# The last twenty microseconds of a two-layer graph and expert network: halves, another order, and two sums on TensorE

## The chip, the cores and the metric

The kernel runs on one core of a Trainium2 chip. The metric is the device time of one launch in microseconds, the median of a few runs. Five engines work side by side, each with its own instruction stream: TensorE (PE, matrix products into PSUM), VectorE (DVE), ScalarE (ACT), GpSimd (POOL) and SyncE (SP, which here only issues DMAs). DMAs issued by SP, ACT and GpSimd run on the core's 16 DMA engines. Semaphores order the engines; a scheduler that knows which instruction reads and writes which tile places the waits.

## The reference

3327 nodes have 256 features each; an adjacency matrix of 3327 x 3327 says which are connected. There are two layers. In each, a normalized `x` goes through a graph step (layer 0 takes the mean of the neighbours, layer 1 weights them by attention) that is added to `x`, and then through a mixture of experts that is added too. In layer 1 the expert part is:

```python
h1 = relu(einsum('bsd,edh->bseh', features, expert_w1) + expert_b1)      # 6 experts, 256 x 256
h2 = relu(einsum('bseh,ehf->bsef', h1, expert_w2) + expert_b2)
expert_out = einsum('bsef,efo->bseo', h2, expert_w3) + expert_b3
sel = take_along_axis(expert_out, top_i[:, :, :, None], axis=2)           # the two best experts of each node
combined = sum(sel * routing_weights[..., None], axis=2)
x = x + combined
```

All is float32. Only two of six experts count for a node, and the kernel computes only those.

## The kernel before

Rows are handled in tiles of 128: 26 tiles, of which the last (tile 25) has 127 rows. `CHUNKS` are groups of four tiles: six whole ones (tiles 0 to 23) and one of two (tiles 24 and 25). `xs` holds `x` of all tiles in SBUF for the whole run.

The stages in time are the graph step of layer 0, its experts, the graph step of layer 1, and its experts. In the expert stage a node's row appears twice, once for each of its experts. The rows of an expert are taken in *slots* of 256 rows. For a slot GpSimd gathers the rows (`rows_in`, line 601), TensorE transposes them (`turned`, line 618), and two layers follow (`layer1`, line 1306, with ScalarE's ReLU at line 1309). `out1` is the third: eight matmul records (four float32 matmuls, two records each) write both 128-row halves `h` of a PSUM tile `ps` (line 1318), VectorE adds the bias `b3` to the whole tile (line 1321) and multiplies each half by the rows' routing weights (line 1323). `rows_out` (line 627) lets GpSimd scatter the two halves with one indirect DMA each into a DRAM array `zd`. `zd` has 2 rows of 256 numbers a node, one for each of its experts. `slots1` is the loop over the slots; `USUAL1` is the number of slots that the data usually needs (29), and if it needs more, a conditional block (`with more(...)`, line 1428) that is usually skipped runs the rest.

The end of the kernel adds up `x` and both rows of `zd`. `results` (line 647) loads a piece of `zd` on SP's queue into a tile `z` of [128, tiles, 2, 256]; `summed` (line 657) lets VectorE add `xs` to the first row, and then the second row to it, both in place; `stored` (lines 662 and 666) writes the sum to the output, and splits the tile of 127 rows into 112 and 15 rows (`last_rows`). `LOW`, the first four chunks (tiles 0 to 15), is done while the last slots still run, because the rows of those nodes are written early. The other ten tiles (16 to 25) follow the last slot: lines 1435 to 1439. They are five pieces of two tiles, 512 KB each, loaded, added and stored in the order of the tiles, the loads on SP's queue and the stores on ACT's.

Every engine keeps the order in which its instructions are given out. Within the code behind the conditional block the order is that of the program. Loads of `zd` wait for all scatters into it, and for what GpSimd does on the skipped block. Whoever reads a PSUM tile waits for the matmuls that write it. `bank(c, shape)` (line 607) takes a tile of one of three pools of PSUM, each with two buffers; a [128, 2, 256] float32 tile takes a whole bank. `ident` is the 128 x 128 identity that the transposes use too.

Of the kernel before, what the change touches and what calls it, by code (L numbers as in the profile page):

```python
# [9 lines left out]
F32 = mybir.dt.float32  # L10
# [5 lines left out]
OP = mybir.AluOpType  # L16
# [3 lines left out]
P = 128  # L20
# [5 lines left out]
def kernel(  # L26
# [26 lines left out]
    nc = tc.nc  # L53
    N, D = x.shape
# [7 lines left out]
    BT = 4  # L62
    CHUNKS = [list(range(t, min(t + BT, NT))) for t in range(0, NT, BT)]
# [8 lines left out]
    def last_rows():  # L72

        n = N - NF * P
        return [(lo, hi) for lo, hi in ((0, n // 16 * 16), (n // 16 * 16, n)) if lo < hi]
# [12 lines left out]
    USUAL1 = min(SLOTS1, int(2 * N / S1 + E1 / 2 + (E1 / 12) ** 0.5))  # L88
    LATE1 = USUAL1 - E1
    KNOWN1 = [n - 4 for n in EARLY1]  # L90
    LOW = CHUNKS[: 4 * len(CHUNKS) // 7]
# [25 lines left out]
    xs = keep.tile([P, NT, D], F32, name="xs")  # L117
# [22 lines left out]
    ident = const.tile([P, P], F32, name="ident")  # L140
# [99 lines left out]
    last = {}  # L240
# [366 lines left out]
    def bank(c, shape):  # L607

        return ps_c[c].tile(shape, F32, name=f"acc{c}") if c >= 0 else ps_mm.tile(shape, F32, name="mm")
# [13 lines left out]
    def rows_out(s, who, y):  # L623
        n = who.shape[1]
        for h in range(n):
            with in_turn_on_pool():
                last["pool"] = nc.gpsimd.indirect_dma_start(  # L627
                    out=zviews[n * s + h], out_offset=bass.IndirectOffsetOnAxis(ap=who[:, h, 0:1], axis=0),
                    in_=y[:, h, :], in_offset=None, bounds_check=2 * NP - 1, oob_is_err=False,
                )  # L630
            if s < LATE1:
                z_ready.append(last["pool"].ins.name)

    def weight(who, h):

        return who.bitcast(F32)[:, h, 2:3]
# [3 lines left out]
    def results(blk, zp, low=None, z=None, behind=(), step=BT):  # L640

        z = zp.tile([P, BT, 2, D], F32, name="z") if z is None else z
        of, case = (zd, {}) if low is None else (zd_low, dict(cond=low, bounds_check="skip_entire_dma"))
        for i in range(0, len(blk), step):
            part = blk[i : i + step]
            n, t0 = len(part), part[0]
            ins = nc.sync.dma_start(z[:, i : i + n], of[2 * t0 * P : 2 * (t0 + n) * P, :].rearrange("(t p k) d -> p t k d", p=P, k=2), **case)  # L647
            if low is not None:
                for name in (*z_ready, *behind):
                    tc.add_manual_dep(ins.ins, name, mybir.DependencyInfo(mybir.DependencyClass.Sync, mybir.DependencyReason.DATA))  # L650
        return z

    def summed(blk, z):

        n, t0 = len(blk), blk[0]
        for k in range(2):
            nc.vector.tensor_tensor(z[:, :n, 0, :], z[:, :n, k, :], z[:, :n, 0, :] if k else xs[:, t0 : t0 + n, :], op=OP.add)  # L657

    def stored(engine, blk, z):
        full = [t for t in blk if t < NF]  # L660
        if full:
            engine.dma_start(
                out[full[0] * P : (full[-1] + 1) * P, :].rearrange("(t p) d -> p t d", p=P), z[:, : len(full), 0, :]
            )
        for lo, hi in last_rows() if blk[-1] >= NF else ():
            engine.dma_start(out[NF * P + lo : NF * P + hi, :], z[lo:hi, len(full), 0, :])
# [300 lines left out]
    early = {}  # L967
# [30 lines left out]
    WB, BB = 3 * 2 * H1, 3 * 2 * H1 + D  # L998
# [110 lines left out]
    who = {}  # L1109
# [186 lines left out]
    def weights1(s, i):  # L1296
        return early["w"][s % 3][:, i * 2 * H1 : (i + 1) * 2 * H1].rearrange("p (k h) -> p k h", k=2)
# [15 lines left out]
    def out1(s, who, h2):  # L1313
        ps = bank(1 if s < EARLY1[1] else 0, [P, 2, D])
        w = weights1(s, 2)
        for h in range(2):
            for c in range(NC1):
                nc.tensor.matmul(ps[:, h, :], h2[:, c, h * P : (h + 1) * P], w[:, c, :],  # L1318
                                 start=(c == 0), stop=(c == NC1 - 1))
        y = early["io"].tile([P, 2, D], F32, name="y", bufs=5)  # L1320
        nc.vector.tensor_tensor(y, ps, early["w"][s % 3][:, None, WB:BB].to_broadcast([P, 2, D]), op=OP.add)  # L1321
        for h in range(2):
            last["dve"] = nc.vector.tensor_scalar(y[:, h, :], y[:, h, :], weight(who, h), None, op0=OP.mult)  # L1323
        outs.append(lambda: rows_out(s, who, y))

    outs = []
    who = {}
    xg, xT, h1, h2, zs = {}, {}, {}, {}, {}
# [14 lines left out]
    def slots1(first, end):  # L1343
        for s in range(first - 3, end + 1):
            if first <= s - 1 < end:
                out1(s - 1, who[s - 1], h2.pop(s - 1))
# [76 lines left out]
    tail = ctx.enter_context(tc.tile_pool(name="tail", bufs=len(CHUNKS)))  # L1423
# [4 lines left out]
    with more(*early["more"]):  # L1428
        list(slots1(USUAL1, SLOTS1))
        for blk in LOW:  # L1430
            z = results(blk, tail)
            summed(blk, z)
            stored(nc.scalar, blk, z)

    zs = [(blk, results(blk, tail, step=2)) for blk in CHUNKS[len(LOW) :]]
    for blk, z in zs:
        for i in range(0, len(blk), 2):
            summed(blk[i : i + 2], z[:, i : i + 2])
            stored(nc.scalar, blk[i : i + 2], z[:, i : i + 2])


# [33 lines left out]
```

## Time and profile before

| | |
|---|---|
| Median of 3 runs | 1002.71 us (1001.34, 1002.71, 1010.84) |
| Profiled execution: time, span | 1003.3 us, 1000.3 us |
| PE busy | 923.2 us, 92% of the span |
| PE weight loads, DVE, ACT, POOL busy | 777.1, 485.0, 280.9, 434.8 us |
| Mean granted clock of TensorE | 0.975 |
| DMA | 200.56 MB, 200 GB/s in the mean; 386 GB/s from 988 to 994.5 us |
| The last slot's matmuls end | 979.1 us |
| The five loads of `zd` are issued | 985.87 to 988.3 us |
| VectorE's adds of the last pieces | 989.60 to 996.60 us |

The span runs from the first to the last instruction of the profiled execution; the time is that of the whole launch, 3.0 us more. Busy time is time in which an engine computes; waiting, and issuing a DMA, are not counted. TensorE is busy almost throughout, but not in the last 21 us, in which it does nothing at all; a share of the whole span says nothing of that stretch. The chain of waits follows what ended last back from step to step. The granted clock is the share of full speed at which TensorE was allowed to run: 1.00 or 0.50 in the stretches of this trace.

### The profile page before, as it was taken

Reading aid. Unit: us, or ns where it says so; the run is one execution under the profiler, and the core shown is the slowest. Engines: PE = TensorE matmul, PEld = TensorE weight load, DVE = VectorE, ACT = ScalarE, POOL = GpSimd, SP = SyncE. Lnnn points to the kernel's source line nnn. Section 1 sums busy time; section 2 is a strip of 40 time slices with the busy share of each in tenths; the row PEclk is TensorE's granted clock in tenths of the full one; section 3 lists DMA queues with packets and bytes.
Section 4 is the critical chain, followed back from the end, with each engine's and each line's share of the span. In section 5 each row is a group of like instructions: output and inputs, shape, how many; then the busy total and the mean of one; then the engine's idle time right before and its main releaser. Section 6 shows DMA issues by size and latency. Waiting matters only on the chain. (4 is left out here: it accounts for less than half of the span.)

```text
span 1000.3 us, 14311 instructions
## 1 busy us (share of the span) xinstructions
PE 923.2 (92%) x4506; PEld 777.1 (78%) x4506; DVE 485.0 (48%) x1788; ACT 280.9 (28%) x634; POOL 434.8 (43%) x407
## 2 busy tenths in 40 slices
PE   7889999989997999999999999999999898789981
PEld 5777878779896999888988687777787787678870
DVE  7564585245622332212122687576666563435563
ACT  3311321035311111111111444152141643234420
POOL 2040052532576455454545311000634677677751
PEclk9999999999999999999999999999999999889986
DMA  9989667856666656567888398988973223242376
GB/s 337 335 277 317 217 177 252 255 173 214 189 159 169 201 157 147 167 191 212 226 268 273 57 320 292 305 276 317 244 215 85 65 75 64 44 102 90 96 253 209
DMA packets 104945, 200.56 MB, mean 200 GB/s; under 512 B 30436, under 2 KB 59558, under 8 KB 104864
## 3 DMA queue, kind: packets, MB, share of 16 engines
q1 hardware_dynamic: 64002, 150.87, 46.1%
q0 software_dynamic: 20528, 30.56, 14.2%
q10 hardware_dynamic: 20334, 18.17, 5.7%
q8 instruction: 36, 0.59, 0.3%
q14 instruction: 45, 0.37, 0.2%
HBM read 170.39 MB, written 35.47 MB: 206 GB/s over the span
## 5 line engine op out<-in xcount | busy, mean ns | idle before, releaser
L831 PE MATMUL acc<-big,y 128*128 128x512 f32 (+2 forms) x1456 | 337.3, 385 | 21.9 <-ACT y L887 7.5
L831 PEld LDWEIGHTS acc<-big,y 128*128 128x128 f32 (+1 forms) x1456 | 260.4, 190 | 79.1 <-issue 8.6
L1065 PE MATMUL acc<-xT,w 128*128 128x256 f32 (+3 forms) x1024 | 211.0, 359 | 0.0
L1065 PEld LDWEIGHTS acc<-xT,w 128*128 128x128 f32 x1024 | 184.0, 198 | 15.8 <-issue 3.5
L384 POOL DMA_INDIRECT list<-where,t_idx x104 | 111.2, 1069 | 155.2 <-DVE t_idx L381 97.0
L705 DVE TENSOR_SCALAR big<-adj 128x1536 fp32r<-128x1536 int32 (+5 forms) x128 | 111.0, 871 | 100.5 <-DMA adj<-in_adj_t 61.5
L1088 PE MATMUL acc<-w,hid 128*128 128x256 f32 (+3 forms) x512 | 118.0, 381 | 0.0
L1095 POOL DMA_INDIRECT xd<-y,who x44 | 68.2, 1550 | 98.9 <-DVE y L1093 53.9
L1073 DVE TENSOR_TENSOR hid<-hid,acc 128x512 f32<-128x512 f32 (+3 forms) x64 | 40.0, 625 | 143.9 <-PE acc L1065 134.8
L1088 PEld LDWEIGHTS acc<-w,hid 128*128 128x128 f32 (+3 forms) x512 | 88.9, 177 | 20.2 <-issue 3.6
L1069 ACT ACTIVATE hid<-acc 128x512 f32<-128x512 f32 (+3 forms) x64 | 35.0, 547 | 202.0 <-PE acc L1065 190.5
L1309 ACT ACTIVATE h<-acc,v 128x256 f32<-128x256 f32 x116 | 54.8, 473 | 93.8 <-PE acc L1306 93.3
L601 POOL DMA_INDIRECT xg<-hd,who x58 | 63.3, 1092 | 40.3 <-issue 35.1
L627 POOL DMA_INDIRECT zd<-y,who x58 | 67.2, 1159 | 29.6 <-issue 12.2
L1306 PE MATMUL acc<-h,v 128*128 128x256 f32 x232 | 61.1, 386 | 1.7 <-ACT h L1309 1.7
L1318 PE MATMUL acc<-v,h 128*128 128x256 f32 x232 | 61.5, 412 | 0.1
L1306 PE MATMUL acc<-xT,v 128*128 128x256 f32 x232 | 61.0, 385 | 0.0
L289 POOL TENSOR_TENSOR ln_var<-ln_var,half 128x2 f32<-128x2 f32 (+2 forms) x19 | 15.9, 839 | 101.1 <-DVE ln_var L287 87.7
L1095 POOL DMA_INDIRECT xd<-y,whos x20 | 32.2, 1612 | 57.8 <-DVE y L1093 43.3
L1321 DVE TENSOR_TENSOR y<-acc,v 128x512 f32<-128x512 f32 x29 | 20.0, 691 | 73.8 <-PE acc L1318 73.8
L1306 PEld LDWEIGHTS acc<-h,v 128*128 128x128 f32 x232 | 44.5, 199 | 9.0 <-ACT h L1309 2.5
L1318 PEld LDWEIGHTS acc<-v,h 128*128 128x128 f32 x232 | 46.3, 210 | 6.6 <-ACTq L575 0.5
(300 smaller groups left out, 987.7 us busy)
## 6 DMA issues: line engine op xcount, KB each, us to landing
adj<-in_adj_t SPq DMA_DIRECT2D x58, 768.0 KB
w<-in_ffn_w SPq DMA_DIRECT2D x78, 512.0 KB
adj<-in_adj_t SPq DMA_DIRECT2D x25, 639.5 KB
adj<-in_adj_t SPq DMA_DIRECT2D x25, 512.0 KB
adj<-in_adj_t SPq DMA_DIRECT2D x12, 767.0 KB
hd<-ln_h ACTq DMA_DIRECT2D x12, 512.0 KB
w_all<-w1d SPq DMA_DIRECT2D x6, 898.0 KB
w1d<-in_ffn_w ACTq DMA_DIRECT2D x18, 256.0 KB
```

The source lines that it names most:

```text
L384: ins = nc.gpsimd.indirect_dma_start(out=rows_of[2 * (t0 + j) + i], out_offset=bass.IndirectOffsetOnAxis(ap=idx[:, i, j : j + 1], axis=0), ...
L601: last["pool"] = nc.gpsimd.indirect_dma_start(out=xg[:, h, :], out_offset=None, in_=of, in_offset=bass.IndirectOffsetOnAxis(ap=who[:, h, 1 ...
L627: last["pool"] = nc.gpsimd.indirect_dma_start(out=zviews[n * s + h], out_offset=bass.IndirectOffsetOnAxis(ap=who[:, h, 0:1], axis=0), in_= ...
L705: last["mask"] = nc.vector.tensor_scalar(mask[:kr, :, :cols], a[:kr, :, :cols], value, None, op0=op)
L831: last["graph"] = nc.tensor.matmul(acc[c][k][:, :w], y[:kr, j, part, k * P : (k + 1) * P], mask[:kr, jj, i0 : i0 + w], start=(j == 0 and p ...
L1065: last["slot"] = nc.tensor.matmul(q[:, c, :n], w[:, k, h0 : h0 + 2 * P - 1 : 2], xT[:, k, :n], start=(k == 0), stop=(k == KD - 1))
L1073: last["silu"], last["hid"] = silu, nc.vector.tensor_mul(hid[:, :, :n], hid[:, :, :n], ps[1][:, :, :n])
L1088: nc.tensor.matmul(ps[:m, h, :], hid[c // 2][:, c % 2, h * P : h * P + m], w3[:, c // 2, c % 2, :], start=(c == 0), stop=(c == NC0 - 1))
L1095: ins = last["pool"] = nc.gpsimd.indirect_dma_start(out=xd_of[2 + h] if s < USUAL0 else xd, out_offset=bass.IndirectOffsetOnAxis(ap=who[s] ...
L1306: ins = nc.tensor.matmul(ps[:, c, :], w[:, k, c : H1 : NC1], src[:, k, :], start=(k == 0), stop=(k == 1))
L1309: last["act"] = nc.scalar.activation(dst[:, c, :], ps[:, c, :], AF.Relu, bias=early["w"][s % 3][:, BB + 2 * i + c : BB + 2 * i + c + 1])
L1318: nc.tensor.matmul(ps[:, h, :], h2[:, c, h * P : (h + 1) * P], w[:, c, :], start=(c == 0), stop=(c == NC1 - 1))
```

## The change

Two places change. In `out1`, for the last usual slot only, the bias add is done in halves, each followed by its half's weighting. At the end, the ten last tiles are taken in another order: the piece with tiles 24 and 25 first, then 20 and 21, 22 and 23, 16 and 17, 18 and 19. Of these five pieces the second and the fourth are summed by TensorE: a matmul of the identity by `xs` starts a PSUM tile, and is placed ahead of the loads; two more add the two rows from `z`; ScalarE copies the sum back into `z`. The others are summed by VectorE as before. The stores of TensorE's pieces are issued by ACT, those of VectorE's by SP. The five loads stay on SP's queue, 512 KB each.

```diff
@@ out1
         y = early["io"].tile([P, 2, D], F32, name="y", bufs=5)
-        nc.vector.tensor_tensor(y, ps, early["w"][s % 3][:, None, WB:BB].to_broadcast([P, 2, D]), op=OP.add)
-        for h in range(2):
-            last["dve"] = nc.vector.tensor_scalar(y[:, h, :], y[:, h, :], weight(who, h), None, op0=OP.mult)
+        for hs in ((0,), (1,)) if s == USUAL1 - 1 else ((0, 1),):
+            part = slice(hs[0], hs[-1] + 1)
+            nc.vector.tensor_tensor(y[:, part, :], ps[:, part, :], early["w"][s % 3][:, None, WB:BB].to_broadcast([P, len(hs), D]), op=OP.add)
+            for h in hs:
+                last["dve"] = nc.vector.tensor_scalar(y[:, h, :], y[:, h, :], weight(who, h), None, op0=OP.mult)
         outs.append(lambda: rows_out(s, who, y))
@@ the end of tile_adj_ffn_kernel
-    zs = [(blk, results(blk, tail, step=2)) for blk in CHUNKS[len(LOW) :]]
-    for blk, z in zs:
-        for i in range(0, len(blk), 2):
-            summed(blk[i : i + 2], z[:, i : i + 2])
-            stored(nc.scalar, blk[i : i + 2], z[:, i : i + 2])
+    parts = [(blk, i) for blk in CHUNKS[:len(LOW) - 1:-1] for i in range(0, len(blk), 2)]
+    sums = {}
+    for n, (blk, i) in enumerate(parts):
+        if n % 2:
+            ps = sums[n] = bank(n // 2 % 2, [P, 2, D])
+            nc.tensor.matmul(ps, ident, xs[:, blk[i] : blk[i] + 2, :], start=True, stop=False)
+    zs = {blk[0]: tail.tile([P, BT, 2, D], F32, name="z") for blk in CHUNKS[len(LOW) :]}
+    for blk, i in parts:
+        results(blk[i : i + 2], tail, z=zs[blk[0]][:, i : i + 2])
+    for n, (blk, i) in enumerate(parts):
+        z = zs[blk[0]][:, i : i + 2]
+        if n in sums:
+            for k in range(2):
+                nc.tensor.matmul(sums[n], ident, z[:, :, k, :], start=False, stop=k == 1)
+            nc.scalar.copy(z[:, :, 0, :], sums[n])
+        else:
+            summed(blk[i : i + 2], z)
+        stored(nc.scalar if n in sums else nc.sync, blk[i : i + 2], z)
```

## The prediction

> **What bounds the kernel now.** I first read the page's chain of work that ended last: everything that the change touches lies in its last 21 of 1000.3 us. Here is that chain in order of time (start, duration, what).
>
> ```profile
> 977.58 1.57 PE acc L1318 x6
> ...
> 979.17 0.70 DVE y L1321
> ...
> 979.90 0.09 DVE y L1323
> ...
> 980.53 0.43 POOL zd L627
> ...
> 981.81 3.73 DMA zd<-y,who
> ...
> 987.89 7.20 DMA z<-zd
> ...
> 995.18 0.70 DVE z L657
> 995.88 0.02 issue
> 995.91 0.69 DVE z L657
> ```
>
> The last slot's matmuls end, VectorE adds the bias and weights the rows, GpSimd issues two scatters one after the other, and only when both are down may the five loads of `zd` start. After the last load VectorE has 1.4 us of adds. Then the timeline's tail (start, duration, engine, line, operation).
>
> ```profile
> 990.93 0.69 DVE L657 TENSOR_TENSOR z<-z,xs 128x512 f32<-128x512 f32 x1
> 991.05 5.93 ACTq L662 DMA_DIRECT2D out_x<-z  x5
> ...
> 992.29 0.69 DVE L657 TENSOR_TENSOR z<-z,xs 128x512 f32<-128x512 f32 x1
> ...
> 993.63 0.69 DVE L657 TENSOR_TENSOR z<-z,xs 128x512 f32<-128x512 f32 x1
> ...
> 995.18 0.69 DVE L657 TENSOR_TENSOR z<-z,xs 128x512 f32<-128x512 f32 x1
> ...
> 997.01 1.19 ACTq L666 DMA_DIRECT2D out_x<-z  x2
> ```
>
> Each piece's first add starts within 0.1 us of its load's landing: the trace's DMA completions have the five at 989.58, 990.90, 992.27, 993.60 and 995.09, one per 1.38 us, and VectorE needs 1.39 us a piece. So arrival sets the pace, not VectorE. The last piece ends with three stores, issued at 996.63, 997.01 and 997.50. The last completion is at 999.15, and the span closes 1.1 us later.
>
> **The change, part by part.** All sums are made in the profiled execution (span 1000.3 us, time 1003.3 us; the median of the runs shown, 1002.71, is 0.6 lower), against the last completion at 999.15.
>
> *Halves.* One bias add of 128x512 (0.69 us) becomes two of 128x256. The nearest row is the 128x256 add from PSUM of line 1250, mean 0.421. The first scatter starts 0.28 us after the first L1323 ended (four slots in a row: 0.276 to 0.277), so it needs only the first half; adding it earlier brings that scatter forward by 0.69 - 0.42 = 0.27. The second follows 1.28 us behind the first on GpSimd (981.81 - 980.53), by when the second half (some 980.7) is long ready. So everything behind moves by **-0.27**. VectorE has one more instruction, with idle time after it. Two bounds. If the scatter waits for the second weighting after all (it started only 0.013 us after that one ended as well), halves cost: 0.42 + 0.04 + 0.27 + 0.46 + 0.35 = 1.54 against 1.34 now, +0.2. If, on the other side, the first half's add needn't wait for the other half's matmuls, it can start at about 978.3, and GpSimd at 979.4 in place of 980.53: -1.15. I don't take that, because both halves are one accumulator tile, and where ScalarE reads half of such a tile the trace shows TensorE waiting for it before it writes the other half:
>
> ```profile
> 975.87 1.14 PE L1306 MATMUL acc<-h,v 128*128 128x256 f32 x4 [0.56 <-ACT h L1309]
> ```
>
> *Loads in the other order.* Five transfers of 512 KB as before on the same queue, so the same landings 0.27 earlier: piece 0 (tiles 24, 25) 989.31, then 990.63, 992.00, 993.33 and 994.82. The two ends that stay, the scatters' landing (984.11) and the time until SP's queue is released (985.55), move along.
>
> *Partial tile first.* Its three stores (0.35 + 0.45 + 0.70 us of issue) leave the end. They are now on SP, behind VectorE's end with piece 0 (about 990.7), and occupy SP to 992.2. The next to use SP is piece 2's store at 993.4: free. SP's loads are all issued by 988. What follows on SP's rings is behind the loads; that costs nothing, as the stores on ScalarE's queue now don't pass them either (the one issued at 991.05 completed at 995.77, after the last load).
>
> *VectorE's branch.* It keeps pieces 0, 2 and 4. Piece 4 lands 994.82, add starts 0.09 later, two adds take 1.42 (995.18 to 996.60 now), store issued at 996.36. A 256 KB store alone has no row: 128 KB took 1.75 us from issue to completion (996.63 to 998.38), 512 KB 3.03 (974.05 to 977.08); between them 2.2. It completes at **998.56**, 0.59 before 999.15.
>
> *TensorE's branch.* Pieces 1 and 3 get a matmul of the identity by `xs` each, issued right after 979.2: 1.7 us in which nobody waits for TensorE. Then two matmuls a piece when its load is down, a copy from PSUM by ScalarE (128x512, 0.586) and ScalarE's store. VectorE is relieved of 2.8 us, which is worth nothing, since arrival sets its pace. The price is on TensorE. A 256-column float32 matmul is two records here, so a 512-column one is four times a 256-column record. What one costs depends on the granted clock:
>
> ```profile
> 958.89 3.63 PE L1318 MATMUL acc<-v,h 128*128 128x256 f32 x8
> ...
> 967.35 1.89 PE L1318 MATMUL acc<-v,h 128*128 128x256 f32 x8
> ```
>
> Records start 0.427 us apart in the first and 0.216 in the second. The granted clock of five stretches (the column PEclk, the third from the end):
>
> ```profile
> 875.80:882.50 6.70, 4.36 (x13) 3.64 (x14) 0.00 (x0) 0.58 (x1) 5.09 (x6) 0.50 0.48 111
> 882.60:957.60 75.00, 72.39 (x356) 63.31 (x354) 38.81 (x59) 31.64 (x64) 58.86 (x53) 1.00 0.37 104
> 957.70:964.40 6.70, 6.00 (x15) 4.86 (x16) 4.07 (x6) 0.72 (x2) 2.64 (x4) 0.50 1.05 391
> 964.60:981.50 16.90, 13.84 (x64) 11.21 (x62) 11.31 (x16) 4.99 (x11) 9.11 (x7) 1.00 0.56 192
> 981.60:1000.20 18.60, 0.00 (x0) 0.00 (x0) 6.69 (x10) 0.00 (x0) 0.97 (x1) 0.50 0.64 223
> ```
>
> The clock halved 2.4 us after the last matmul. TensorE will be idle from 981 to 990.68 and start at half clock. Four matmuls (pieces 1 and 3) are 16 times 0.427 = 6.82 us there, 3.41 at full clock. Full clock came back 4.45 us after the first matmul at 878.14 and 6.11 after that at 958.39; in five shorter half-clock stretches 2.9 to 3.35 after. I take 4.45, the nearest to the middle: 990.68 + 4.45 + (6.82 - 4.45)/2 = 996.32, plus 0.2 until the result can be read, 0.62 for the copy, 0.03 and 2.2 for the store: **999.36**. Piece 3's data (993.33) is there before piece 1 is done at 994.1, so this branch never waits for a load.
>
> [...]
>
> *Sum.* TensorE's branch ends last, at 999.36 against 999.15: **+0.2 us**. -0.27 from the halves and some 0.6 from the partial tile are there, and are eaten by two pieces summed at half clock. 1003.5 on the profiled execution, 1002.9 on the median's footing.
>
> **Rivals.**
> 1. *The clock stays halved to the end of the burst (slower).* Place: the four matmuls from 990.68. If full clock comes only 6.11 us in, the branch ends at 1000.19, +1.0; if not at all, 1000.6, +1.4. It decides against the change from 4.0 us on, where the branch reaches 999.15. For: 6.11 in the last burst of this very stage. Against: 4.45 and the shorter ones. 1003.7 to 1004.1.
> 2. *VectorE's branch ends last.* Full clock by 2.9 us ends TensorE's branch at 998.59, level with piece 4's store: -0.6, 1002.1. For: five stretches of 2.9 to 3.35. Against: there matmuls began right at the start of a stretch, here the burst begins at any point.
> 3. *The halves overlap the matmuls.* Another -0.9 on whichever branch is last: 1001.1 to 1002.0. Against: the wait of 0.56 above.
> 4. *The halves do not do what they say*, the scatter waits for the last weighting: +0.2 in place of -0.27, 1003.4.
>
> **How the numbers follow.** Forecast (TensorE's branch last, full clock between 3 and 6 us) 0.50, rival 1 0.17, rival 2 0.21, rival 3 0.06, rival 4 0.06. The bounds are -1.5 (rivals 2 and 3) and +1.9 (1 and 4); a 256 KB store at 3.03 instead of 2.2 would add 0.8. So 1001.2 to 1005.4 on the median's footing. The runs of before lie 1.4 below and 8.1 above their median, so a median of a few can be off too: I widen the range to 1000.5 to 1006. About 1% is what a measurement of this kernel can tell from no change, and no case comes near 10 us. What I leave for over 1% is a median that falls on a run like the one of 1010.84: slower 0.035, faster 0.015, within 0.95.
>
> **What would show it.** The first scatter some 1.1 us after the bias add could start (979.17), rather than 1.36. Load landings 1.38 apart as now, the first piece being tiles 24 and 25. PE at a granted clock of 0.5 when its sums begin, records 0.85 us apart, and the last ScalarE copy ending near 997.1, after piece 4's last add at 996.3. The last completion belonging to piece 3's store, not piece 4's. I would be wrong if TensorE's burst ran at full clock, if the loads slowed beside SP's stores, or if the first add began before the eighth matmul record.

## The result, and the profile after

| | before | after |
|---|---|---|
| Median of 22 runs each | 1006.67 us (998.63 to 1013.17) | 1006.78 us (998.39 to 1013.29) |
| Ratio after to before | | 1.0005, 95% interval 0.998 to 1.003 |
| Profiled execution: time, span | 1003.3, 1000.3 us | 1009.49, 1007.7 us |
| Tail in the profile | 21.1 us | 22.2 us |

The change makes no difference that these runs can tell. The *tail* of this section and the following ones is the stretch that the change touches: from the start of the last slot's bias add on VectorE (979.17 and 985.50 us) to the end of the span. Times "in the tail" count from that start. The 6.3 us by which the two starts differ lie ahead of all changed code.

The chain of waits of the changed kernel, in order of time (start, duration, what), is the counterpart of the chain shown before:

```profile
985.50 0.04 DVE y L1323
...
985.84 0.41 DVE y L1323
986.25 0.12 DVE y L1325
...
988.07 3.74 DMA zd<-y,who
...
992.14 3.86 DMA z<-zd
996.00 1.55 issue
997.55 6.13 PE acc L1450 x8
1003.69 0.02 issue
1003.71 0.59 ACT z L1451
```

The chain no longer ends with VectorE's adds after the last load. It goes through a load, 6.1 us of matmuls and ScalarE's copy. The load in it is the first piece's (issued 992.14, landed 996.00). The sums wait for the second piece's: it was issued at 992.63 and landed at 997.36, inside the 1.55 us that the chain calls "issue". The timeline of the same stretch shows both branches:

```profile
985.50 0.76 DVE L1323 TENSOR_TENSOR y<-acc,v 128x256 f32<-128x256 f32 x2 [2.77 <-PE acc L1318]
986.17 0.60 DVE L1325 TENSOR_SCALAR y<-y,who 128x256 f32<-128x256 f32 x2
986.79 0.97 POOL L627 DMA_INDIRECT zd<-y,who  x1 [1.79 <-DVE y L1325]
...
1002.38 0.69 DVE L657 TENSOR_TENSOR z<-z 128x512 f32<-128x512 f32 x1
...
1003.71 0.59 ACT L1451 COPY z<-acc 128x512 f32<-128x512 f32 x1 [1.78 <-PE acc L1450]
1004.33 0.38 ACTq L662 DMA_DIRECT2D out_x<-z  x1
```

VectorE's last add ends at 1003.07, ScalarE's last copy at 1004.30. The first line also shows something that the prediction did not expect: both bias adds of the halves run first (x2), and then both weightings. The windows of the tail, with the granted clock in the third column from the end:

```profile
985.50:992.20 6.70, 1.96 (x4) 0.68 (x4) 1.28 (x4) 0.00 (x0) 1.95 (x2) 1.00 0.10 34
992.30:1002.40 10.10, 4.85 (x6) 2.18 (x7) 3.48 (x6) 0.59 (x1) 0.00 (x0) 0.50 0.87 310
1002.50:1005.80 3.30, 1.17 (x3) 0.19 (x1) 0.57 (x1) 0.59 (x1) 0.00 (x0) 1.00 0.66 225
```

Full clock came back at 1002.49, 4.94 us after the first of the sums' records at 997.55.

### The profile page after: what moved, and what is told of

It reads as the page before. It is cut to its first block, busy times and chain, and to the rows that moved or that the text cites. A ratio compares the mean times of both kernels' runs of the same rounds, so it can differ in the third digit from the quotient of the medians.

```text
span 1007.7 us, 14342 instructions
## 1 busy us (share of the span) xinstructions
PE 937.9 (93%) x4518; PEld 784.9 (78%) x4518; DVE 482.4 (48%) x1785; ACT 282.3 (28%) x636; POOL 435.5 (43%) x407
## 3 DMA queue, kind: packets, MB, share of 16 engines
q0 software_dynamic: 20528, 30.56, 14.2%
## 5 line engine op out<-in xcount | busy, mean ns | idle before, releaser
L831 PE MATMUL acc<-big,y 128*128 128x512 f32 (+2 forms) x1456 | 344.0, 391 | 23.8 <-DVE big L705 14.9
L831 PEld LDWEIGHTS acc<-big,y 128*128 128x128 f32 (+1 forms) x1456 | 265.2, 194 | 82.9 <-issue 16.3
L1088 PEld LDWEIGHTS acc<-w,hid 128*128 128x128 f32 (+3 forms) x512 | 88.9, 177 | 20.3 <-issue 3.6
L627 POOL DMA_INDIRECT zd<-y,who x58 | 69.4, 1196 | 25.5 <-issue 12.2
L1323 DVE TENSOR_TENSOR y<-acc,v 128x512 f32<-128x512 f32 (+1 forms) x30 | 20.1, 672 | 77.5 <-PE acc L1318 77.5
```

The source lines that it names most:

```text
L627: last["pool"] = nc.gpsimd.indirect_dma_start(out=zviews[n * s + h], out_offset=bass.IndirectOffsetOnAxis(ap=who[:, h, 0:1], axis=0), in_= ...
L831: last["graph"] = nc.tensor.matmul(acc[c][k][:, :w], y[:kr, j, part, k * P : (k + 1) * P], mask[:kr, jj, i0 : i0 + w], start=(j == 0 and p ...
L1088: nc.tensor.matmul(ps[:m, h, :], hid[c // 2][:, c % 2, h * P : h * P + m], w3[:, c // 2, c % 2, :], start=(c == 0), stop=(c == NC0 - 1))
```

## The experiments

A whole run scatters by more than ten microseconds, so the kernels are judged by the tails of their profiles. All numbers of this table are places in the tail, in us; "last load" counts from the issue of the first load.

| kernel | tail | first scatter | last load | VectorE's last add ends | ScalarE's last copy ends | last store down |
|---|---|---|---|---|---|---|
| before | 21.1 | 1.36 | 9.22 | 17.4 | | 20.0 |
| e1 before again | 21.1 | 1.36 | 9.16 | 17.4 | | 19.9 |
| changed | 22.2 | 1.29 | 9.49 | 17.6 | 18.8 | 21.0 |
| e5 changed again | 21.5 | 1.29 | 9.28 | 17.4 | 18.0 | 20.3 |
| e2 all on VectorE | 20.5 | 1.29 | 9.12 | 17.2 | | 19.4 |
| e3 clock kept | 21.4 | 1.29 | 9.18 | 17.3 | 17.2 | 20.2 |
| e4 order alone | 20.7 | 1.36 | 9.20 | 17.3 | | 19.5 |
| e6 halves in order | 20.9 | 1.09 | 9.27 | 17.2 | | 19.7 |
| e7 one piece on TensorE | 21.5 | 1.29 | 9.25 | 17.5 | 16.6 | 20.3 |
| e8 all together | 20.2 | 1.09 | 9.23 | 17.0 | | 19.2 |
| e9 e7, a store on SP | 21.2 | 1.29 | 9.79 | 17.9 | 16.3 | 20.1 |
| e10 first and third | 21.9 | 1.29 | 10.52 | 18.6 | 17.4 | 20.7 |
| e11 e9 again | 21.2 | 1.29 | 9.05 | 17.6 | 16.7 | 20.0 |
| e12 e10 again | 21.5 | 1.29 | 9.19 | 17.3 | 17.3 | 20.2 |

### Does the tail repeat?

e1 is the kernel before, unchanged.

> The kernel before once more, for the spread of the tail. Tail here and below: from the start of the last slot's bias add on VectorE to the end of the span; 21.1 us in the profile of before (979.2 to 1000.3), 22.2 in that of the changed kernel (985.5 to 1007.7). Theory 1 (what differs between executions lies ahead of the tail, in stretches at half clock, and the tail itself repeats): 20.8 to 21.4, while the start of the tail can lie anywhere from 975 to 992. Rival (the tail itself varies by a microsecond from execution to execution, and the 1.1 us between the two profiles says nothing): below 20.5 or over 21.7.

The tail was 21.1 us again (21.06 against 21.12), while it began at 987.9 instead of 979.2. So for this kernel one profile gives the tail to some 0.1 us, and what differed between its two executions lies ahead of it. Two profiles are few, and kernels with sums on TensorE repeat less well: theirs differ by 0.06 to 0.7 us (e5, e11, e12).

### Without the sums on TensorE

```diff
-        if n % 2:
+        if False:
             ps = sums[n] = bank(n // 2 % 2, [P, 2, D])
...
-        stored(nc.scalar if n in sums else nc.sync, ...)
+        stored(nc.scalar if n % 2 else nc.sync, ...)
```

> The changed kernel, but VectorE sums all five pieces; order, halves and the two store queues as changed. Theory 1 (TensorE's sums at half clock end last; VectorE is paced by the arrival of the loads and can sum five pieces as fast as three): tail 21.1 to 21.4, 0.9 shorter than the changed kernel's 22.2; VectorE's last add ends 17.5 to 17.7 after the bias add began, as in the changed kernel. Rival (VectorE needs the relief; with five pieces it falls behind the loads): last add later by 0.5 or more, tail 22 or more. Rival 2 (the stores on SP's queue are what costs, not TensorE): tail unchanged, 22.0 to 22.4.

The tail fell to 20.5, below the kernel before. VectorE's adds of the five pieces in the timeline of e2:

```profile
1005.26 0.69 DVE L657 TENSOR_TENSOR z<-z,xs 128x512 f32<-128x512 f32 x1
...
1008.72 0.69 DVE L657 TENSOR_TENSOR z<-z 128x512 f32<-128x512 f32 x1
1009.33 0.69 DVE L657 TENSOR_TENSOR z<-z,xs 128x512 f32<-128x512 f32 x1
1010.05 0.69 DVE L657 TENSOR_TENSOR z<-z 128x512 f32<-128x512 f32 x1
```

The last add ends at 17.2, not later than with two pieces fewer (17.6 and 17.4). VectorE needed no relief. Theory 1 holds, and its number was too careful: 20.5 where 21.1 to 21.4 was expected, since the last load landed 0.4 earlier than in the changed kernel's first profile. Rival 2 falls: the two store queues are still there.

### With TensorE's clock kept up

```diff
+    spare = bank(2, [P, 2, D])
+    for _ in range(9):
+        nc.tensor.matmul(spare, ident, xs[:, 0:2, :], start=True, stop=True)
     for n, (blk, i) in enumerate(parts):
```

> The changed kernel with nine more identity matmuls into an unused PSUM bank between the two early ones and the sums, so that TensorE doesn't fall idle before the sums (the nine add nothing to the result; they are work that only keeps it busy for some 8 us). Theory 1 (the half clock is what makes TensorE's branch the last): records of the sums 0.43 us apart instead of 0.85, the last copy of ScalarE ends some 2 us after piece 3's load has landed instead of 4.2, VectorE's branch is the last, tail 21.1 to 21.4. Rival (what costs are the waits and the way over PSUM and ScalarE, not the clock): tail 22.0 or more with records at 0.43.

The timeline of e3 has the sums at full speed (four records in 1.96 us; the changed kernel had eight in 6.12):

```profile
1007.21 1.96 PE L1453 MATMUL acc<-z,ident 128*128 128x512 f32 x4 [0.78 <-issue]
...
1009.85 1.98 PE L1453 MATMUL acc<-z,ident 128*128 128x512 f32 x4 [0.69 <-DMA z<-zd]
...
1011.88 0.58 ACT L1454 COPY z<-acc 128x512 f32<-128x512 f32 x1 [2.09 <-PE acc L1453]
1012.49 0.44 ACTq L662 DMA_DIRECT2D out_x<-z  x1
```

Records are 0.43 us apart, and ScalarE's last copy ends at 17.2 instead of 18.8: against that profile of the changed kernel, the half clock was 1.6 us of TensorE's branch. Against its second profile (e5, below, copy to 18.0) it was 0.9. The copy ended 2.65 us after piece 3's load had landed, where I had said 2 and left the copy out. The tail, 21.4, lies at the end of what was expected, and still 0.9 above e2. Here both branches are ready together, and their last two 256 KB stores are issued at 17.18 and 17.29; they took 2.69 and 2.88 us instead of the 2.14 of e2's last one. So the clock is one price of TensorE's sums and two stores that meet at the end are a second.

### The order of the pieces alone

```diff
-    zs = [(blk, results(blk, tail, step=2)) for blk in CHUNKS[len(LOW) :]]
...
+    parts = [(blk, i) for blk in CHUNKS[:len(LOW) - 1:-1] for i in range(0, len(blk), 2)]
...
+        summed(blk[i : i + 2], z)
+        stored(nc.scalar, blk[i : i + 2], z)
```

> The kernel before with the pieces in the other order alone: VectorE sums all, ScalarE's queue stores all, no halves. Theory 1 (the partial tile's three stores at the end cost 0.6, as predicted): tail 20.4 to 20.7. Rival (the last 256 KB store takes as long from its issue as the three small ones, which overlap): tail 21.0 to 21.3. If the loads land as early after their issue as before (the last one 9.2 us after the first was issued, against 9.5 in the changed kernel), the stores on SP's queue were what slowed them; if 9.5 again, it wasn't them.

Tail 20.7: taking the partial tile first is worth 0.4 us of the 21.1, somewhat less than the 0.6 foreseen. The last store, issued at 17.37, was down 2.15 later; before, three stores issued at 17.46, 17.84 and 18.33 were down by 20.0. e2 has the halves (0.07) and the second store queue besides and ends 0.16 earlier, so the second queue alone brought some 0.1, no more than two profiles of one kernel may differ. The order wasn't quite alone: the fifth load was issued at 10.52 in the tail, instead of 8.71. It landed no later for that: the loads took 9.20, as before and as in e2 with stores on SP, so in these profiles SP's stores didn't slow them.

### The changed kernel once more

> The changed kernel once more. Theory 1: TensorE's branch is the last again, and what moves the tail is the moment at which full clock comes back: 4.9 us after the first sum's record in the first profile, tail 22.2; with that moment called u, tail = 22.2 + (u - 4.9)/2, so 21.2 to 22.9 for u of 2.9 to 6.2, and VectorE's last add ends at 17.2 to 17.6 as in the other runs. Rival (22.2 came from the loads, which landed 0.3 later there than in every other run): tail 20.5 to 21.0.

Full clock came back 3.30 us after the first record, and the tail was 21.5, where the formula gives 21.4. TensorE's branch was the last again (copy to 18.0, VectorE to 17.4). The rival's number didn't come true: the last load landed 0.2 earlier than in the first profile, but the tail was not 20.5 to 21.0. So two profiles of the same kernel differ by 0.7, for the most part with the moment of the clock. Full clock came back 4.94, 3.30, 3.96, 3.73 and 4.34 us after the first record in the five profiles in which it did during or after the sums (the changed kernel, e5, e9, e10, e12). What sets that moment is not shown. In the traces of before and of the changed kernel, each of the 18 stretches at half clock that end before the run does lasts 3.41, 6.83 or 10.24 us (13, 4 and 1 of them), one, two or three times 3.41; the five delays scatter over 1.6 us.

### The halves alone, with their order set

```diff
+            with tc.issue_after(last["dve"].ins) if hs == (1,) else nullcontext():
                 nc.vector.tensor_tensor(y[:, part, :], ps[:, part, :], ...)
```

This stands in the kernel before, together with the halves of the change.

> The kernel before with the halves alone, and the second half's bias add queued on VectorE behind the first half's weighting (add, weight, add, weight; the changed kernel has add, add, weight, weight). Theory 1 (a scatter waits only for its own half, and the order of four VectorE instructions decides what the halves bring): first scatter 1.09 after the bias add began, instead of 1.36 before and 1.29 in the changed kernel, second 2.37, first load issued at 6.43, tail 20.8. Rival 1 (the scatter waits for both halves): first scatter at 1.5 or later, tail 21.2 or more. Rival 2 (the first half's add starts ahead of the last matmul): first scatter before 1.0, or the eighth matmul record beginning after the first add.

The timeline of e6:

```profile
1034.85 0.38 PE L1318 MATMUL acc<-v,h 128*128 128x256 f32 x1
1035.26 0.42 DVE L1324 TENSOR_TENSOR y<-acc,v 128x256 f32<-128x256 f32 x1 [2.77 <-PE acc L1318]
1035.72 0.35 DVE L1326 TENSOR_SCALAR y<-y,who 128x256 f32<-128x256 f32 x1
1035.99 0.42 DVE L1324 TENSOR_TENSOR y<-acc,v 128x256 f32<-128x256 f32 x1
1036.35 0.97 POOL L627 DMA_INDIRECT zd<-y,who  x1 [1.59 <-DVE y L1326]
```

Add, weight, and the first scatter is issued at 1.09, while the second half is still being added. Both scatters and the first load (6.42) come 0.27 earlier than before, as foreseen to the hundredth, and the tail is 20.9. Both rivals fall: the scatter needs its own half only, and the first add begins after the last matmul record. The changed kernel gets 0.07 of the 0.27, because the scheduler put the second bias add ahead of the first weighting, which has to wait for the first add anyway.

### One piece on TensorE, and whose queue the stores stand in

```diff
-        if n % 2:
+        if n == 1:
...
-        stored(nc.scalar if n in sums else nc.sync, ...)
+        stored(nc.scalar if n % 2 else nc.sync, ...)
```

So the fourth piece, now VectorE's, is still stored by ScalarE.

> The changed kernel with only the second piece summed by TensorE, the fourth by VectorE. Theory 1 (two pieces in a row at half clock are what is late; one is done in 4 records of 0.85 us): ScalarE's copy ends at some 16.0 to 16.3, its store is down by 18.6, VectorE's branch is the last, tail 20.4 to 20.8 as with all pieces on VectorE (20.5). Rival (any use of TensorE here holds up the others, by its early matmuls or its waits): tail 21.3 or more.

TensorE's piece was done well before the end (copy to 16.6, its store down at 18.8, 0.3 and 0.2 later than expected), and yet the tail was 21.5, as the rival said. The timeline of e7 shows why:

```profile
1055.58 0.69 DVE L657 TENSOR_TENSOR z<-z 128x512 f32<-128x512 f32 x1
1056.11 0.58 ACT L1451 COPY z<-acc 128x512 f32<-128x512 f32 x1 [17.69 <-DMA z<-zd]
...
1056.72 0.91 ACTq L662 DMA_DIRECT2D out_x<-z  x2
1056.91 0.69 DVE L657 TENSOR_TENSOR z<-z 128x512 f32<-128x512 f32 x1
```

The first line is the fourth piece's last add, done at 16.2. Its store is the second of the two in the third line: on ScalarE's queue it stood behind the copy and the store of TensorE's piece until 17.15. It then ran beside the last piece's store, which took 2.79 us. VectorE itself was 0.3 later than in e2, because the first load was issued 0.2 later.

> As e7_one_on_tensor, but the fourth piece's store is issued by SP instead of ScalarE's queue, where in e7 it stood behind the copy and the store of TensorE's piece (issued at 17.15 of the tail, though VectorE had the sum at 16.2). Theory 1 (the queue in order is what made e7 late: two 256 KB stores then ran at once): that store issued at 16.0 to 16.3, the last store takes 2.1 to 2.3 instead of 2.8, tail 20.4 to 20.9. Rival (one piece on TensorE already costs by itself): tail 21.2 or more.

With that store on SP (`nc.scalar if n in sums else nc.sync`), it was issued at 16.55, earlier than in e7 but later than the 16.0 to 16.3 expected, and the last one took 2.19, as theory 1 says. But the tail was 21.2, not 20.4 to 20.9: the loads came late this time, the last one 9.79 after the first issue. e11 is the same kernel again.

> e9_one_store_on_sp once more, since its loads came late (the last landed 9.8 us after the first issue, 9.1 to 9.3 in the runs without TensorE). Theory 1 (late loads there were chance, not TensorE's doing): last load 9.1 to 9.3 after the first issue, tail 20.4 to 20.9. Rival (with TensorE reading pieces while loads run, loads are slowed): 9.5 or more again, tail over 21.

The loads were on time (9.05), so their lateness in e9 was not TensorE's doing each time; but the tail was 21.2 again, for another reason: the first load was issued at 7.10 instead of 6.63. If those two delays (0.6 and 0.5) are taken off, 20.6 to 20.7 remains, nearly the 20.5 of e2; that is arithmetic, not a run. In all three profiles with one piece on TensorE (21.5, 21.2, 21.2) the rival's number came true, and none of the six profiles without such sums has its last load down as late (15.9 in the tail at most, 16.1 to 16.4 in these three). So it is shown that the store's queue cost e7 time, but not that one piece on TensorE is free otherwise.

### The first and the third piece on TensorE

```diff
-        if n % 2:
+        if n in (0, 2):
```

> The changed kernel with TensorE on the first and third piece instead of the second and fourth; the stores go with the engine, as there. Theory 1 (the price is a burst of fixed length, some 6 us at half clock and back, that began 1.35 too late; the first and third pieces land 1.35 earlier): TensorE's branch is down at 19.0 to 19.7, VectorE's is the last, tail 20.4 to 20.9. Rival (stores of both engines at the end get in each other's way whichever comes first): tail 21.2 or more.

TensorE's branch was down at 19.7 and VectorE's was the last, as theory 1 says, but only at 20.7, so that the tail was 21.9: the last load took 10.52. e12 is the same kernel again.

> e10_first_and_third once more. There 15 of the 16 parts of the last load had landed by 16.3 of the tail and the sixteenth at 17.1, after an instruction fetch of 16 KB that took one DMA engine 1.0 us at 14.2. Theory 1 (it was the fetch, which does not always fall there): without one among the loads, last load 9.1 to 9.3 after the first issue, TensorE's branch down at 19.3 to 19.9, tail 20.4 to 21.0; with one, a straggler again. Rival (this order of work slows the loads itself): 9.8 or more without a fetch.

The loads took 9.19, as without TensorE, so this order of work need not slow them; but the tail was 21.5, not 20.4 to 21.0. The timeline of e12:

```profile
1000.13 0.36 ACTq L662 DMA_DIRECT2D out_x<-z  x1
...
1000.53 1.17 ACTq L666 DMA_DIRECT2D out_x<-z  x2
...
1001.88 0.58 ACT L1451 COPY z<-acc 128x512 f32<-128x512 f32 x1 [1.78 <-DMA out_x<-z]
1002.49 0.47 ACTq L662 DMA_DIRECT2D out_x<-z  x1
```

The first piece holds the partial tile, so ScalarE now issues its three stores, and the second copy starts only behind them, at 16.7; the eighth record had begun at 15.78, and in the changed kernel the copy began 0.6 after the last record did (1003.08 to 1003.71). The last store of this branch is issued at 17.32, that of VectorE's at 17.30, and they take 2.89 and 2.40, so that TensorE's branch was down at 20.2 and not at 19.3 to 19.9. The rival (stores of both engines meet at the end) describes this run better than theory 1. Starting the burst 1.35 us earlier gained little: 0.3 were lost again on ScalarE's queue, and some 0.7 where the two stores met (2.89 instead of the changed kernel's 2.17).

### A version made of the parts that paid

```diff
+    blk, i, _ = parts.pop()
+    parts += [(blk, i, 1), (blk, i + 1, 1)]
...
+        summed(blk[i : i + m], z)
+        stored(nc.scalar if n % 2 else nc.sync, blk[i : i + m], z)
```

It has no sums on TensorE, and the halves in the order of e6.

> A version made of what the runs showed: no sums on TensorE, halves with the order of e6_halves_in_order, the changed kernel's order of pieces and two store queues, and the last piece loaded, summed and stored as two single tiles (256 KB loads, 128 KB stores). Theory 1: 0.2 from the order of the halves and 0.8 from the shorter end of the last piece (an add of 0.42 instead of 0.69 twice, and a 128 KB store of 1.75 us instead of 2.14) against 20.5: tail 19.3 to 19.8, 2.5 shorter than the changed kernel's and 1.6 shorter than before. Rival (the end is set by the DMA engines, which still have the other stores to do): tail 20.2 or more. By the whole time no theory expects a verdict: 0.2% is less than the interval of 0.5% that 22 runs gave.

The tail was 20.2, the shortest of all: 0.9 less than before and 0.3 less than e2. That is 0.4 more than expected; the rival's number came true, but not for its reason alone. The timeline of e8:

```profile
1044.65 0.69 DVE L657 TENSOR_TENSOR z<-z 128x512 f32<-128x512 f32 x1
1045.26 0.75 DVE L657 TENSOR_TENSOR z<-z,xs 128x256 f32<-128x256 f32 x2
...
1045.92 0.75 DVE L657 TENSOR_TENSOR z<-z 128x256 f32<-128x256 f32 x2
```

VectorE was still busy with the fourth piece when the first single tile landed (15.01 in the tail; its add starts at 15.60). It then made both tiles' first adds ahead of the second ones, and the last ended at 17.0, not at the 16.5 that the arrivals would allow. Here, for once, VectorE is the bound at the end. Both tiles were stored only then: the two 128 KB stores were issued together, at 17.05, and took 1.98 and 2.16, not 1.75. So of the 0.8 expected of the split last piece hardly 0.1 came; the 0.2 of the halves did. By the whole time, nothing is shown: the ratio to the kernel before is 1.0037, with an interval from 0.9993 to 1.0081.

## Why the prediction was right or wrong

**The forecast of no change** was right: +0.2 us was forecast, the medians of 22 runs differ by +0.1, and the ratio's interval lies within 1% on both sides. That agreement is no proof of the 0.2, which no whole run could show; the tails are what the steps are judged by.

**The time itself missed the range.** 1006.78 lies 0.8 above 1006. The step that failed is the footing: "1002.9 on the median's footing", and, in how the numbers follow, "I widen the range to 1000.5 to 1006". The footing was the median of three runs. With 22, the kernel before has 1006.67: the forecast was off by 3.9 us and its footing by 4.0, so the change has no share in the miss. One of the three runs had stood at 1010.84, and I took it for the exception. The 22 runs of before have a standard deviation of 4.7 us; by that, the median of three is uncertain by some 3 us (1.25 times 4.7 divided by the root of 3). A range that is to hold in 8 cases of 10 needs about 4 us upwards on that alone; the range had the bounds of the cases and 0.6 more.

What moves the runs lies ahead of the tail. In the ten profiles taken where the kernel before ran in some 1000 to 1015 us, the tail began between 978.8 us (e10, with 24 us at half clock ahead of it) and 995.3 (e3, with 55); the correlation of the two is 0.89. Over the 22 runs of the changed kernel, time and mean granted clock have -0.82. Beside e5 to e8 the kernel before, too, took some 5% longer (1054.06), and the tails began at 1020 to 1040 with 61 to 82 us at half clock; there TensorE also waited longer (42.6 us idle in the last expert stage of e8, 21.9 in e1). Half clock goes with waiting TensorE, so the correlation doesn't say which comes first. Why the kernels took longer at that time was not settled.

**TensorE's branch last**: right in both profiles of the changed kernel, with records 0.85 us apart at a granted clock of 0.50, and e2 and e3 tell its price. Its size was off. Foreseen was its last store down at 20.19 in the tail (999.36), measured 20.99: the sums began 0.54 late (0.21 of it from the halves, 0.18 from the loads, the rest in the wait after the landing), and full clock came after 4.94 instead of 4.45 us (0.25). The copy and its store took what was said (0.59, and 2.17 against 2.2). The tail was 1.1 longer than before in one profile and 0.4 in the other, not 0.2. The first went the way of rival 1, of which full clock at 4.94 is the mild form. In e5 full clock came after 3.30 us, sooner than the 4.45 foreseen, which is worth 0.58; that was eaten by sums that began 0.58 late.

**The halves, -0.27**: the mechanism was right and e6 shows the number, but the changed kernel got -0.07. The step "adding it earlier brings that scatter forward by 0.69 - 0.42 = 0.27" took the program's order for VectorE's. That the code behind the conditional block runs in program order is no warrant for `out1`, which stands ahead of it.

**Partial tile first, and VectorE's branch**: VectorE's branch was put 0.59 before 999.15. e2 is that branch without the other: last store down at 19.36 in the tail, 0.62 before the 19.98 of before. The agreement is partly luck: the halves gave 0.2 less, and loads 0.1 faster (9.12 against 9.22), a shorter wait after the last landing and a store of 2.14 instead of 2.2 made up for it. In the changed kernel itself this branch was down at 20.0, 0.65 later than foreseen, and in e5 at 19.6.

**Relief of VectorE is worth nothing**: right, by e2.

**ScalarE's queue** is what the prediction left out. It priced TensorE's branch, and didn't ask what stands behind the copy on ScalarE's queue, nor what two last stores do to each other. In the changed kernel itself this cost nothing much (last stores 1.2 us apart, 0.7 in e5); in e3, e7 and e12 it decided.

## What to carry to other kernels

Giving an idle engine a share of the last work pays only if the engine that has it now is what is late; here the arrival of the loads was, and the idle engine came with half its clock (records 0.85 us apart instead of 0.43), an extra copy (0.59 us), and another queue. If parts of an edit are to act in a certain order on one engine, look at that engine's instructions, for the program's order may not be the one that runs. And where whole runs scatter by 1%, judge an edit of the last 20 us by that stretch alone, and take the level from many runs, not three.

## What was not expected of the hardware

**A store whose packets came late.** In the kernel before, ScalarE had issued stores from 991.05 on while SP's loads were under way. What the DMA queues moved between 991.1 and 993.8 us (packets, MB, share of the 16 engines):

```profile
DMA packets 525, 1.01 MB, mean 374 GB/s; under 512 B 32, under 2 KB 32, under 8 KB 525
## 3 DMA queue, kind: packets, MB, share of 16 engines
q1 hardware_dynamic: 525, 1.01, 102.8%
```

q1 carries SP's loads; ScalarE's q10 does not appear. The store issued at 991.05 was down at 995.77, after the last load; one of half its size, issued at 996.63 when the loads were through, needed 1.75 us. In e7 and in the changed kernel (issue at 1001.96), where the loads were through as well, q10's first packet came 0.9 us after the issue; here it came at 994.2, 3.2 us after. So for these 2.7 us the loads' queue alone moved data, with a store issued on another queue. Whether that store's packets already stood in their queue then, the trace doesn't say. On SP's own queue a store came behind the loads as well: in the changed kernel the one issued at 997.47 had its first packet at 1000.38, 2.9 us after, and the loads' last packet ended at 1001.15.

**Instruction fetches.** A packet of 16 KB of kind "instruction" took 0.96 to 1.33 us of one DMA engine in some tails. e11, from 2.3 to 5.8 of the tail, where the last scatters go down:

```profile
q0 software_dynamic: 96, 0.22, 19.2%
q8 instruction: 1, 0.02, 2.4%
```

There it came at 2.7: 15 of the 16 parts of the first scatter had landed by 3.70, the last landed at 5.18, and the first load was issued 0.5 late. In e7 one came at 2.6, the last part landed at 4.91, and the first load was 0.2 late. In e10 it came at 14.2, 15 of the 16 parts of the last load had landed by 16.3, and the last part at 17.1. In e12 one came at 2.5, and the first scatter's last part landed at 4.59, still before the second scatter was down (4.87), so it did no harm. Seven of the eight profiles with sums on TensorE have such a packet between 0.4 us ahead of the tail and 15.7 in it, none of the six without has one before 21. Whose instructions they were the trace doesn't say, and no run was made to find out. So these delays may be a price of the added work on TensorE, but that is not shown; late loads as in e9 occurred without one.

**Half clock with TensorE fully busy.** The same stretch of the first graph step, before and after the change, in windows (columns: PE, PEld, DVE, ACT, POOL busy with their counts, granted clock, DMA share, GB/s). The kernel before:

```profile
162.90:169.60 6.70, 6.70 (x43) 5.66 (x43) 5.36 (x37) 0.51 (x2) 0.00 (x0) 1.00 0.73 264
```

The changed kernel, whose code is the same there:

```profile
156.00:162.80 6.80, 6.79 (x48) 5.96 (x47) 2.34 (x7) 1.10 (x3) 0.00 (x0) 1.00 1.07 344
162.90:169.60 6.70, 6.70 (x23) 5.84 (x24) 3.73 (x22) 0.38 (x2) 0.00 (x0) 0.50 0.60 222
```

TensorE was busy without a gap in both windows, and yet ran 23 matmul records in the second, at half clock, where the other execution ran 43. e2 and e4 have the same stretch at half clock within a microsecond of that place, and e12 has it 2.4 us earlier; before, e1 and e3 don't. What halved the clock there stays open.
